# Selective scan beside full attention: some products with C move to VectorE, which sums them over a unit

## The chip, the cores and the metric

The kernel runs on one core of a Trainium2 chip. The metric is the time of one execution in device microseconds. The engines of the core are named as in the profile: PE (TensorE, matrix products), DVE (VectorE), ACT (ScalarE), POOL (GpSimd) and SP (SyncE, which here issues most of the DMAs).

## The reference

A tensor of 8 images, 64 channels, 64 x 64 pixels passes through four layers: full attention over all 4096 pixels of an image, two blocks of windowed attention, a convolution with filters made from the data, and a layer around a selective scan. Two pieces matter here. The attention of layer 0:

```python
scores = jnp.einsum('bdn,bdm->bnm', Q, Q) / c ** 0.5      # 4096 x 4096 per image
prob = jax.nn.softmax(scores, axis=-1)
out = jnp.einsum('bnm,bdm->bdn', prob, V)
```

And the scan of layer 3, over 4096 positions in four directions k, with 16 states n for each of 128 channels:

```python
def step(h, inp):
    u_t, dt_t, B_t, C_t = inp
    h = h * jnp.exp(dt_t[..., None] * A) + dt_t[..., None] * B_t[:, :, None, :] * u_t[..., None]
    return (h, jnp.einsum('bkcn,bkn->bkc', h, C_t))
```

The output y of a position is thus the sum over 16 states of h times C. All numbers are fp32.

## The kernel before, in words

**Pairs and what runs together.** The images are taken in four pairs p. `tile_kernel` (lines 1906 to 1915) calls `scans(p, ...)` for each pair and gives it other work to run beside it: the back stage of pair p-1 (`back`, after the scan) and the front stage of pair p+1 (`front`: layers 0, 1 and 2 and the sources of the scan). Layer 0 of pairs 0 and 1 is done before the first scan, in `begin`. So full attention (`layer0`, lines 1291 to 1320) runs beside the scan only twice: that of pair 2 beside the scans of pair 1, and that of pair 3 beside the scans of pair 2.

**The scan.** A unit is one image, one direction k and one chunk c of 512 positions: 2 x 4 x 8 = 64 units a pair, of 8 steps each, and a step holds two states, j = 0 and 1. So a pair has 512 steps. The directions of an image are numbered in order by `nth`, 0 to 3.

- `inputs` (line 1688) loads the unit's xs by DMA on SP, makes the step sizes and u (lines 1697 to 1704: two ACT passes, a DVE product) and writes the rows of B and C to memory. It is called for the next unit during step 1 of a unit.
- `fetch` (1712) loads a step's rows of B and C, broadcast to 128 partitions, on SP, with three buffers each. `products` (1719) has GpSimd multiply B with u into `vd`, which has six buffers.
- `step` (1724): for each state ACT makes the decay `dad` in PSUM (line 1743; tag "da", three buffers, shared with what `inputs` needs); DVE scans (1746), either into `hd` in SBUF or in place into `dad`; ACT copies the last column into `carry` (1754); and the product with C is written to `vd` (1757 or 1760). `own`, line 1732, says how many of a step's two products DVE makes, those of the last states. GpSimd makes the others, [...] only DVE's own states are scanned in place. For pairs 0 to 2 `own` is 0 in even steps (one GpSimd product of 1024 elements) and 1 in odd ones; for pair 3 it is 1, in every fourth step 2.
- `sums` (1764) adds the 16 products of a unit in one PSUM bank `yd` (tag "y", one buffer) by multiplying each with the identity on PE (line 1775), one step behind, and placed by `net.behind` after the next step's product `st["w"]`. After the eighth step DVE takes the bank into `Y` (1784, 1786), or for `nth` 3 into `yo` (1789, one buffer), which is stored by a DMA on SP (1790).

**The attention.** For each chunk jc of 512 columns, 32 blocks t: for both images of the pair PE makes scores (1305) into PSUM banks "f" (three buffers), ACT takes their exponential into `e` (1311, six buffers), and PE multiplies the previous block's `e` with the values into `po` (1297, one bank). DVE copies `po` out after the 32 blocks (1320).

**The order.** Each piece of beside-work yields a cost: 2.2 for one block t, 4 for one of the 8 groups of values before the loop. `scans` lets it advance, after each step, by an equal share of the planned cost over 512 - 24 steps (line 1681). The planned cost is that of the front stage (its yields add up to 2016) and a quarter of it for the back stage (whose yields add up to 264.4). This sets the order in which instructions are written. The framework then orders them for each engine by priority and readiness at compile time and adds the semaphores. A tile whose buffer is taken waits for the last use of the tile that had it. [...]

Of the kernel before, what the change touches and what calls it, by code (L numbers as in the profile page):

```python
# [9 lines left out]
F32 = mybir.dt.float32  # L10
AF = mybir.ActivationFunctionType
ALU = mybir.AluOpType
# [3 lines left out]
B, C, HH, WW = 8, 64, 64, 64  # L16
L = HH * WW
P = 128
# [6 lines left out]
TD = 512  # L25
# [1132 lines left out]
class _Direct:  # L1158
# [8 lines left out]
    def __init__(self, net, ctx):  # L1167
        self.net, self.tc, self.nc, self.w = net, net.tc, net.nc, net.w
        tc = self.tc
        self.dram = ctx.enter_context(tc.tile_pool(name="mem", bufs=2, space=bass.MemoryType.DRAM))  # L1170
        self.slabs = ctx.enter_context(tc.tile_pool(name="slabs", bufs=3))
        self.ps = ctx.enter_context(tc.tile_pool(name="ps_scan", bufs=3, space=PSUM))
        self.pf = ctx.enter_context(tc.tile_pool(name="ps_front", bufs=3, space=PSUM))
        self.kept = {}
        self.turn = -1

    def begin(self, ctx):

# [91 lines left out]
    def layer0(self, p):  # L1270


        nc, tc, w, net, half = self.nc, self.tc, self.w, self.net, self.HALF
        X = self.flat("X")
        nc.sync.dma_start(X, self.net.x[2 * p : 2 * p + 2].rearrange("b c h w -> (b c) (h w)"))
        att = self.padded("att")
        VT = self.flat("VT").rearrange("p (t c) -> p t c", c=P)

        def at(rows, t):
            return X[rows, t * P : (t + 1) * P]  # L1280

        with self.work("w0") as wk:
            for g in range(8):
                pv = self.bank("pval", (P, 4, P))
                nc.tensor.matmul(pv, lhsT=net.ones[0:1, :], rhs=net.b1row.rearrange("o a c -> o (a c)").unsqueeze(1).to_broadcast([1, 4, P]), start=True, stop=False)
                for j in range(4):
                    nc.tensor.matmul(pv[:, j, :], lhsT=at(slice(0, P), 4 * g + j), rhs=net.w1bd, start=False, stop=(j == 3))
                nc.scalar.activation(VT[:, 4 * g : 4 * g + 4, :], pv, AF.Relu)
                yield 4

            parts = wk.tile([P, 2, 32, NCH], F32, name="parts", tag="parts", bufs=1)
            for jc in range(NCH):
                po = self.total("po")

                def weigh(t, es):
                    for im in range(2):
                        nc.tensor.matmul(  # L1297
                            po[half[im]], lhsT=VT[:, t, half[im]], rhs=es[im], start=(t == 0), stop=(t == 31)
                        )

                last = None
                for t in range(32):
                    ss = [self.bank(f"s{im}") for im in range(2)]
                    for im in range(2):
                        nc.tensor.matmul(  # L1305
                            ss[im], lhsT=at(half[im], t), rhs=X[half[im], jc * CH : (jc + 1) * CH], start=True, stop=True
                        )
                    es = []
                    for im in range(2):
                        e = wk.tile([P, CH], F32, name="e", tag="e", bufs=6)  # L1310
                        nc.scalar.activation(  # L1311
                            e, ss[im], AF.Exp, scale=C**-0.5, accum_out=parts[:, im, t, jc : jc + 1]
                        )
                        es.append(e)
                    if last is not None:
                        weigh(*last)
                    last = (t, es)
                    yield 2.2
                weigh(*last)
                nc.vector.tensor_copy(self.rows(att, jc), self.img(po))  # L1320

            sums = net.sums[:, p]
            nc.vector.tensor_reduce(sums, parts, AX.X, ALU.add)
            rec = wk.tile([P, 2, 32], F32, name="rec", tag="rec", bufs=1)
            nc.vector.reciprocal(rec, sums)
            for g in range(8):
                pr = self.bank("prec")
                for j in range(4):
                    for im in range(2):
                        nc.tensor.matmul(  # L1330
                            pr[half[im], j * P : (j + 1) * P],
                            lhsT=rec[:, im, 4 * g + j : 4 * g + j + 1].to_broadcast([P, 64]),
                            rhs=w["ident"],
                            start=True,
                            stop=True,
                        )
                d = self.rows(att, g)
                nc.vector.tensor_tensor(d, d, self.img(pr), ALU.mult)
                yield 4
        with self.work("w0b") as wk:  # L1340
            for c in range(NCH):
                acc = self.bank("cacc", (P, 8, 64))
                yield from self.dwconv(acc, att, 8 * c, 8, w["dw2"], None)
                cv = wk.tile([P, 8, 64], F32, name="cv", tag="cv")
                nc.scalar.activation(cv, acc, AF.Relu, scale=net.bn23[:, 0:1], bias=net.bn23[:, 1:2])
                pw = self.bank("pw")
                nc.tensor.matmul(pw, lhsT=w["w3bd"], rhs=cv, start=True, stop=True)
                t = wk.tile([P, CH], F32, name="t", tag="t")
                nc.scalar.activation(t, pw, AF.Identity, scale=net.bn23[:, 2:3], bias=net.bn23[:, 3:4])
                x = X[:, c * CH : (c + 1) * CH]  # L1350
                nc.vector.tensor_tensor(x, x, t, ALU.add)
                yield 3
        return X
# [370 lines left out]
    def step(self, i, st):  # L1724

        nc, w, net = self.nc, self.w, self.net
        wk, ps = self.sw, self.ps
        u = self.units[i // 8]
        k, c, at, CC, v = u["k"], u["c"], u["at"], st["C"], st["v"]

        n0 = 2 * (i % 8)
        own = 1 + (i % 4 == 3) if u["image"] >= B - 2 else i % 2
        rev = k >= 2

        def along(t):
            return t[:, ::-1] if rev else t

        h = wk.tile([P, 2 - i % 2, TD], F32, name="hd", tag=f"h{i % 2}", bufs=1)
        hs = []
        for j in range(2):  # L1740
            n = n0 + j
            da = self.bank("dad", (P, TD), "da")
            nc.scalar.activation(da, u["du"][:, 0], AF.Exp, scale=net.As[:, k, n : n + 1])  # L1743
            first = 0.0 if at == 0 else self.carries[:, n : n + 1]
            to = da if j >= 2 - own else h[:, j]
            nc.vector.tensor_tensor_scan(along(to), along(da), along(v[:, j]), first, ALU.mult, ALU.add)  # L1746
            hs.append(to)
            if at < NTD - 1 and (own or j):
                ends = h[:, :, 0] if rev else h[:, :, TD - 1]
                cs = self.carries[:, n0 : n0 + 2]  # L1750
                if own:
                    ends = to[:, 0:1] if rev else to[:, TD - 1 : TD]
                    cs = self.carries[:, n : n + 1]
                nc.scalar.activation(cs, ends, AF.Copy)  # L1754

        if own == 0:
            st["w"] = nc.gpsimd.tensor_tensor(v, h, CC, ALU.mult)  # L1757
        for j in range(2 if own else 0):
            engine = nc.vector if j >= 2 - own else nc.gpsimd
            m = engine.tensor_tensor(v[:, j], hs[j], CC[:, j], ALU.mult)  # L1760
            if j == 0:
                st["w"] = m

    def sums(self, i, st, after=None):

# [1 line left out]
        wk, ps = self.sw, self.ps  # L1767
        u = self.units[i // 8]
        k, c = u["k"], u["c"]
        if i % 8 == 0:  # L1770
            u["y"] = ps.tile([P, TD], F32, name="yd", tag="y", bufs=1)
        y = u["y"]
        for j in range(2):
            n = 2 * (i % 8) + j
            m = nc.tensor.matmul(y, lhsT=w["ident"], rhs=st["v"][:, j], start=(n == 0), stop=(n == NST - 1))  # L1775
            if after is not None and j == 0:
                net.behind(m, after)
        if i % 8 < 7:
            return

        yd = net.part(self.Y, k, c)
        yp = y.rearrange("p (a b) -> p a b", b=64)
        if u["nth"] == 0:
            nc.vector.scalar_tensor_tensor(yd, self.img(u["x"]), net.dsum, yp, ALU.mult, ALU.add)
        elif u["nth"] < 3:
            nc.vector.tensor_tensor(yd, yd, yp, ALU.add)
        else:
            o = wk.tile([P, TD], F32, name="yo", tag="yo", bufs=1)
            nc.vector.tensor_tensor(self.img(o), yd, yp, ALU.add)
            nc.sync.dma_start(u["out"][:, c * TD : (c + 1) * TD], o)  # L1790

# [155 lines left out]
```

## Time and profile before

| | |
|---|---|
| runs, median (lowest to highest) | 13679.33 us (13679.1 to 13687.01) |
| the profiled execution, its time | 13724.29 us |
| its span | 13722.5 us |
| its mean granted PE clock | 0.88 |
| busy in the span | PE 11044.8, DVE 8484.9, ACT 7083.5, POOL 8012.5 us |
| sums on PE (line 1775) | 8192 instructions, 4620.1 us |
| products with C, POOL, 1024 elements (1757) | 768, 2358 ns each |
| products with C, POOL, 512 elements (1760) | 1152, 1280 ns each |
| products with C, DVE, 512 elements (1760) | 1408, 674 ns each |
| scans, DVE (1746), the largest group | 2352, 1271 ns each |
| store of `yo`, issue to landing | 64, 2.4 us median |

An fp32 matrix product appears as two matmul instructions. Busy time is the time in which an engine had an instruction under way; instructions of PE overlap at their ends. A slice of the page is a fortieth of the span, 343 us, and its digit the busy share in tenths. In a group or a timeline, "out<-in" names the tiles written and read; "idle before, releaser" says what ended the time in which the engine stood still.

### The profile page before, as it was taken

Reading aid. Unit: us, or ns where it says so; the run is one execution under the profiler, and the core shown is the slowest. Engines: PE = TensorE matmul, PEld = TensorE weight load, DVE = VectorE, ACT = ScalarE, POOL = GpSimd, SP = SyncE. Lnnn points to the kernel's source line nnn. Section 1 sums busy time; section 2 is a strip of 40 time slices with the busy share of each in tenths; the row PEclk is TensorE's granted clock in tenths of the full one; section 3 lists DMA queues with packets and bytes.
Section 4 is the critical chain, followed back from the end, with each engine's and each line's share of the span. In section 5 each row is a group of like instructions: output and inputs, shape, how many; then the busy total and the mean of one; then the engine's idle time right before and its main releaser. Section 6 shows DMA issues by size and latency. Waiting matters only on the chain. (4 is left out here: it accounts for less than half of the span.)

```text
span 13722.5 us, 141112 instructions
## 1 busy us (share of the span) xinstructions
PE 11044.8 (80%) x46358; PEld 4075.2 (30%) x46358; DVE 8484.9 (62%) x9891; ACT 7083.5 (52%) x15475; POOL 8012.5 (58%) x3983
## 2 busy tenths in 40 slices
PE   9999986888786669979888677997898766766665
PEld 2243322334232222224432222223453222222221
DVE  0121336777668673366666766337666778998985
ACT  5556515565536545555554545555554554454442
POOL 0000005888878754566666785556656687877882
PEclk9999977998898889988898788998889888888887
DMA  0000005666667753454555664435545577778882
GB/s 24 1 1 1 3 14 191 237 236 229 219 214 253 248 170 129 143 173 165 173 176 181 234 242 149 139 134 184 182 160 171 192 247 262 270 241 278 294 298 97
DMA packets 706252, 2385.19 MB, mean 174 GB/s; under 512 B 81120, under 2 KB 81248, under 8 KB 704480
## 3 DMA queue, kind: packets, MB, share of 16 engines
q1 hardware_dynamic: 681312, 2319.76, 49.5%
q10 hardware_dynamic: 24192, 56.29, 1.1%
q8 instruction: 367, 6.01, 0.2%
q14 instruction: 381, 3.12, 0.1%
HBM read 2272.97 MB, written 102.76 MB: 173 GB/s over the span
## 5 line engine op out<-in xcount | busy, mean ns | idle before, releaser
L1722 POOL TENSOR_TENSOR vd<-B,du 128x1024 f32<-128x1024 f32 x2048 | 4833.6, 2367 | 3890.9 <-DMA B<-rows 2485.1
L1775 PE MATMUL yd<-vd,pack 128*128 128x512 f32 x8192 | 4620.1, 695 | 1323.4 <-POOL vd L1757 576.6
L1746 DVE TENSOR_TENSOR_SCAN hd<-dad,carry,vd 128x512 f32<-128x512 f32 x2352 | 2948.5, 1271 | 933.8 <-ACT dad L1743 483.4
L1743 ACT ACTIVATE dad<-du,As 128x512 f32<-128x512 f32 x4096 | 2721.0, 680 | 1142.8 <-DVE hd L1746 730.6
L1775 PEld LDWEIGHTS yd<-vd,pack 128*128 128x128 f32 x8192 | 1621.4, 214 | 3993.6 <-issue 1786.3
L1757 POOL TENSOR_TENSOR vd<-hd,C 128x1024 f32<-128x1024 f32 x768 | 1810.6, 2358 | 1204.1 <-DVE hd L1746 599.6
L1311 ACT ACTIVATE e<-s 128x512 f32<-128x512 f32 x2048 | 1199.9, 591 | 1012.2 <-PE s L1305 1010.4
L1760 POOL TENSOR_TENSOR vd<-hd,C 128x512 f32<-128x512 f32 x1152 | 1473.8, 1280 | 339.7 <-DVE hd L1746 281.1
L1746 DVE TENSOR_TENSOR_SCAN dad<-dad,carry,vd 128x512 f32<-128x512 f32 x1232 | 1562.0, 1274 | 124.4 <-POOL vd L1722 73.2
L1305 PE MATMUL s<-X 64*128 64x512 f32 x4096 | 1324.4, 648 | 79.7 <-ACT e L1311 79.5
L1297 PE MATMUL po<-e,VT 128*64 128x512 f32 x4096 | 1194.9, 627 | 13.2 <-ACT e L1311 13.2
L1760 DVE TENSOR_TENSOR vd<-dad,C 128x512 f32<-128x512 f32 x1408 | 939.3, 674 | 66.5 <-ACT carry L1754 57.7
L1754 ACT ACTIVATE carry<-hd 128x1 f32<-128x1 f32 (+1 forms) x1680 | 334.8, 202 | 1012.0 <-DVE hd L1746 1007.8
L1305 PEld LDWEIGHTS s<-X 64*128 64x128 f32 x4096 | 360.1, 187 | 958.9 <-issue 785.8
L1459 PEld LDWEIGHTS w_av<-vals,w_e 64*64 64x64 f32 x16384 | 556.6, 147 | 195.7 <-issue 84.3
L1459 PE MATMUL w_av<-vals,w_e 64*64 64x9 f32 x16384 | 584.7, 208 | 25.7 <-ACT w_e L1449 25.5
L1444 DVE TENSOR_TENSOR w_e<-w_s,bias 128x512 f32<-128x512 f32 x512 | 329.8, 682 | 443.1 <-PE w_s L1432 442.2
L1754 ACT ACTIVATE carry<-dad 128x1 f32<-128x1 f32 x1232 | 208.7, 169 | 697.7 <-DVE dad L1746 695.1
L1697 PE MATMUL pdd<-xs,xdt 128*128 128x512 f32 x512 | 341.7, 755 | 205.5 <-DVE hd L1746 85.8
L1449 ACT ACTIVATE w_e<-w_e 128x512 f32<-128x512 f32 x512 | 311.6, 627 | 376.2 <-DVE w_e L1444 262.2
L1746 DVE TENSOR_TENSOR_SCAN hd<-dad,vd 128x512 f32<-128x512 f32 x336 | 400.5, 1211 | 164.5 <-ACT dad L1743 75.5
L1297 PEld LDWEIGHTS po<-e,VT 128*64 128x64 f32 x4096 | 221.4, 136 | 822.1 <-issue 771.9
(247 smaller groups left out, 10634.9 us busy)
## 6 DMA issues: line engine op xcount, KB each, us to landing
B<-rows SPq DMA_DIRECT2D x2048, 512.0 KB, 5.0
C<-rows SPq DMA_DIRECT2D x2048, 512.0 KB, 4.5
xs<-xt SPq DMA_DIRECT2D x128, 256.0 KB, 3.3
xs<-xc SPq DMA_DIRECT2D x128, 256.0 KB, 3.8
xc<-xcv ACTq DMA_DIRECT2D x64, 256.0 KB, 3.4
zs<-z ACTq DMA_DIRECT2D x64, 256.0 KB, 3.6
xt<-XT ACTq DMA_DIRECT2D x32, 512.0 KB, 7.6
rows<-bc SPq DMA_DIRECT2D x256, 64.0 KB, 1.8
```

Of the source, the lines that this page charges most:

```text
L1297: nc.tensor.matmul(po[half[im]], lhsT=VT[:, t, half[im]], rhs=es[im], start=(t == 0), stop=(t == 31))
L1305: nc.tensor.matmul(ss[im], lhsT=at(half[im], t), rhs=X[half[im], jc * CH : (jc + 1) * CH], start=True, stop=True)
L1311: nc.scalar.activation(e, ss[im], AF.Exp, scale=C**-0.5, accum_out=parts[:, im, t, jc : jc + 1])
L1459: nc.tensor.matmul(self.av[half[im], x % 4 + j, h, :], lhsT=es[h // 4][half[im], j, h % 4, :], rhs=V[half[im], x + j, h, :], start=True, s ...
L1697: nc.tensor.matmul(pd, lhsT=net.xdt[:, k, :], rhs=x, start=True, stop=True)
L1722: self.nc.gpsimd.tensor_tensor(v, st["B"], dx.to_broadcast([P, 2, TD]), ALU.mult)
L1743: nc.scalar.activation(da, u["du"][:, 0], AF.Exp, scale=net.As[:, k, n : n + 1])
L1746: nc.vector.tensor_tensor_scan(along(to), along(da), along(v[:, j]), first, ALU.mult, ALU.add)
L1754: nc.scalar.activation(cs, ends, AF.Copy)
L1757: st["w"] = nc.gpsimd.tensor_tensor(v, h, CC, ALU.mult)
L1760: m = engine.tensor_tensor(v[:, j], hs[j], CC[:, j], ALU.mult)
L1775: m = nc.tensor.matmul(y, lhsT=w["ident"], rhs=st["v"][:, j], start=(n == 0), stop=(n == NST - 1))
```

## The change

A flag `dense` is 1 while the loop of full attention over jc is being written, else 0. Steps written with the flag set have `own` one higher: in even steps GpSimd makes one product and VectorE one, in odd steps VectorE makes both. So three of each four products are VectorE's. In these steps VectorE's products no longer go into `vd` for PE. The first of a unit is written to a new tile `ysum` (one buffer, SBUF); each later one is written over its state in `dad` in PSUM and then added to `ysum` by a second VectorE instruction. `to_y` lists what PE still has to sum: GpSimd's products, and at the unit's eighth step `ysum`. The accumulation on PE begins with the first of these. Separately, and in all units with `nth` 3, the tile `yo` is gone: the output is written over the unit's xs tile (two buffers) and stored from there.

```diff
@@ layer0
             parts = wk.tile([P, 2, 32, NCH], F32, name="parts", tag="parts", bufs=1)
+            self.dense = 1
             for jc in range(NCH):
...
+            self.dense = 0
             sums = net.sums[:, p]
@@ step
-        own = 1 + (i % 4 == 3) if u["image"] >= B - 2 else i % 2
+        own = 1 + (i % 4 == 3) if u["image"] >= B - 2 else i % 2 + self.dense
...
         for j in range(2 if own else 0):
-            engine = nc.vector if j >= 2 - own else nc.gpsimd
-            m = engine.tensor_tensor(v[:, j], hs[j], CC[:, j], ALU.mult)
-            if j == 0:
-                st["w"] = m
+            if j < 2 - own or not self.dense:
+                engine = nc.vector if j >= 2 - own else nc.gpsimd
+                m = engine.tensor_tensor(v[:, j], hs[j], CC[:, j], ALU.mult)
+            elif "sum" not in u:
+                s = u["sum"] = wk.tile([P, TD], F32, name="ysum", tag="ysum", bufs=1)
+                m = nc.vector.tensor_tensor(s, hs[j], CC[:, j], ALU.mult)
+            else:
+                m = nc.vector.tensor_tensor(hs[j], hs[j], CC[:, j], ALU.mult)
+                nc.vector.tensor_tensor(u["sum"], u["sum"], hs[j], ALU.add)
+            st.setdefault("w", m)
+        st["to_y"] = [v[:, j] for j in range(2) if not self.dense or j < 2 - own]
+        if i % 8 == 7 and "sum" in u:
+            st["to_y"].append(u["sum"])
@@ sums
-        if i % 8 == 0:
-            u["y"] = ps.tile([P, TD], F32, name="yd", tag="y", bufs=1)
-        y = u["y"]
-        for j in range(2):
-            n = 2 * (i % 8) + j
-            m = nc.tensor.matmul(y, lhsT=w["ident"], rhs=st["v"][:, j], start=(n == 0), stop=(n == NST - 1))
+        srcs = st["to_y"]
+        for j, v in enumerate(srcs):
+            start = "y" not in u
+            if start:
+                u["y"] = ps.tile([P, TD], F32, name="yd", tag="y", bufs=1)
+            stop = i % 8 == 7 and j == len(srcs) - 1
+            m = nc.tensor.matmul(u["y"], lhsT=w["ident"], rhs=v, start=start, stop=stop)
             if after is not None and j == 0:
                 net.behind(m, after)
...
-            o = wk.tile([P, TD], F32, name="yo", tag="yo", bufs=1)
+            o = u["x"]
             nc.vector.tensor_tensor(self.img(o), yd, yp, ALU.add)
             nc.sync.dma_start(u["out"][:, c * TD : (c + 1) * TD], o)
```

More of the change, by code (lines that the diff above doesn't have):

```diff
@@ L1320, in layer0 @@
                 nc.vector.tensor_copy(self.rows(att, jc), self.img(po))
+            self.dense = 0
             sums = net.sums[:, p]
@@ L1779, in sums @@
             return
+        y = u["y"]
         yd = net.part(self.Y, k, c)
```

## The prediction

> **What bounds the kernel now.** I read the page first (engine shares, slices, largest groups), then the busy time of each engine in 500 us windows, then the windows in which the full attention runs beside the scan, and there the groups, the waits and the timeline. The change acts only there, so that stage decides and not the average.
>
> The page, engines by slice:
>
> ```profile
> PE   9999986888786669979888677997898766766665
> DVE  0121336777668673366666766337666778998985
> PEclk9999977998898889988898788998889888888887
> ```
>
> Slices 15 to 17 and 25 to 27 stand out: PE at 9 while VectorE falls to 3. The score matmuls of the attention (line 1305) run from 5084.4 to 5980.6 and from 8428.4 to 9321.8 us there. Windows cut at these places (columns: busy time and count of PE, weight load, DVE, ACT, POOL; then clock, DMA share, GB/s):
>
> ```profile
> 5084.40:5983.90 899.50, 853.40 (x2542) 232.62 (x2542) 334.27 (x317) 511.35 (x1466) 456.85 (x222) 0.97 0.40 135
> 8394.40:9323.00 928.60, 878.76 (x2643) 246.67 (x2643) 351.16 (x333) 522.15 (x1485) 482.36 (x235) 0.97 0.41 141
> ```
>
> PE is busy 95% of the first stage, DVE 37%, ACT 57%, POOL 51%. The same windows for line 1775 alone, the summing matmuls with the identity:
>
> ```profile
> 5084.40:5983.90 899.50, 227.55 (x438) 78.18 (x438) 0.97 0.40 135
> 8394.40:9323.00 928.60, 240.34 (x464) 82.22 (x463) 0.97 0.41 141
> ```
>
> A quarter of PE's time is this sum. One fp32 product is two matmul instructions, so 219 products in 227.55 us: 1.04 us each. 219 is 109.5 steps of two products, which agrees with the planned costs (below). Who waits, in the first stage:
>
> ```profile
> ACT e L1311 <- PE s L1305: 270.7, 160, 5.5
> POOL vd L1722 <- PE yd L1775: 268.0, 57, 8.2
> DVE Y L1786 <- PE yd L1775: 230.5, 12, 26.9
> ...
> PE s L1305 <- ACT e L1311: 39.4, 27, 3.5
> ```
>
> ACT, POOL and DVE all wait for PE, DVE up to 26.9 us in one piece; PE waits 39.4 us for ACT and hardly for anything else. PE's timeline where nothing disturbs it:
>
> ```profile
> 5599.55 1.13 PE L1305 MATMUL s<-X 64*128 64x512 f32 x4
> 5600.61 1.08 PE L1297 MATMUL po<-e,VT 128*64 128x512 f32 x4
> 5601.62 1.13 PE L1305 MATMUL s<-X 64*128 64x512 f32 x4
> ...
> 5609.74 1.12 PE L1697 MATMUL pdd<-xs,xdt 128*128 128x512 f32 x2
> 5610.80 1.04 PE L1706 MATMUL pbc<-xs,pack 128*32 128x512 f32 x2
> 5611.77 1.13 PE L1305 MATMUL s<-X 64*128 64x512 f32 x4
> ```
>
> One block t of the attention takes 2.07 us (start to start), the inputs of a unit 2.03 us. So a stage needs at least 256 x 2.07 = 530, plus 218 sums x 0.99 = 216 (the timeline's block of two lasts 1.98), plus 14 x 2.03 = 28: 774 us. It takes 899.5. The 125 us between are PE's losses: waits for ACT and stretches at a lower clock.
>
> [...]
>
> **The change part by part.**
>
> *Which steps.* A pair's plan is 504 + 2016 = 2520 cost over 488 steps, 5.164 a step. The attention's loop costs 256 x 2.2 = 563.2, hence 109 steps, and begins after 264.4 for the back stage and 32 for the values: the flag holds in steps 58 to 166 of pairs 1 and 2, units 7 to 20. Pairs 0 and 3 never see it.
>
> *Removed on PE.* A whole unit has 5 products (4 from GpSimd, one for the sum) in place of 16; the first and last unit are partly flagged. Counted over steps 58 to 166: 149 products fewer per pair, 149 x 1.04 = 155 us. PE sets the stage's end, so this counts in full: 899.5 - 155 = 744.5.
>
> *Moved to VectorE.* VectorE's products rise from 54 to 163, +109 x 0.674 = 73 us. 149 additions and 14 first products into the sum; the nearest row for the addition is line 1789 (PSUM plus SBUF into SBUF), 678 ns: 101 us. The product is now written to PSUM; scans into PSUM (1274 ns) and into SBUF (1271) say that costs nothing. The dearest bound for both is line 1786 with its strided operand, 1064 ns; then the addition's group alone grows to 159 us. VectorE goes from 334 to 509 us of about 745, 68%: covered by PE, with 236 us of slack. Without that cover the 175 us would be paid in full.
>
> *GpSimd.* 54 products of 512 go (1.27 us) and 55 shrink from 2.35 to 1.27: -128 us, 457 to 329. It was waiting anyway; worth nothing.
>
> *ScalarE.* An even step copies two carries separately where it copied one pair: some 48 more copies of 0.17 to 0.2 us, 9 us a stage. ScalarE goes to 520 of 745, 70%. Here I charge something. The sum blocks, 2 us each, are where ScalarE does the scan's exponentials without delaying the attention's: after a score pair it has 2.07 - 1.26 = 0.8 us free, and one exponential takes 0.68. With fewer sum blocks more of them fall into the attention's own loop, and PE waits. I let the 125 us of losses grow as ScalarE's share, 70/57: +29 us a stage. Ends: losses 40 lower, since the scan's bursts are spread wider by VectorE's longer work, to 100 higher.
>
> *The new waits.* The sum tile has one buffer. VectorE's first product of a unit waits until PE has consumed the previous unit's sum; behind it on VectorE's queue stand the scans, for which ScalarE (three PSUM buffers) waits, and behind that the attention's exponentials. PE's sum in turn waits for the unit's last addition. VectorE already meets PE once a unit at the Y update, up to 26.9 us early, so this meeting is mostly the same one. A unit holds VectorE for 16 x 1.27 + 12 x 0.674 + 11 x 0.678 + 2 = 38 us against PE's 47 at its floor: 9 us of slack; I put nothing on it beyond the 29.
>
> *Output from the xs buffer.* In 64 units the result is written over xs and stored from there. The load of xs two units on now waits for that store to land (2.4 us median), and on SP's queue the B and C loads stand behind it. In the trace the xs load often follows the store by 1 to 4 us, and its consumer comes 10 us later or more, so 1 us or so each is late and mostly covered. Bounds 0 to 64 x 2.4 = 154 us; I take 5.
>
> *Sum.* 2 x (155 - 29) - 5 = 247 us. Against the profiled execution: 13722.5 - 247 = 13475 span. That execution (13724.3 with what lies around the span) is 45 us above the runs' median 13679.33, 0.33%; I carry the difference over: 13679 - 247 = 13432, say 13430.
>
> **Rivals.**
>
> *A, PE-bound stage, as summed.* 13310 to 13500. The lower end: each stage's losses fall by 30 us in place of growing by 29, 370 off; the upper: they grow by 60 to 65.
>
> *B, ScalarE and the clock take half.* If PE waits at every scan exponential (109 x 2 x 0.5 us = 109 a stage less what already waits) or the clock falls from 0.97 to 0.88, as in windows with 84% PE (745 x 0.1 = 75 us a stage), the gain is about 2 x 70: 13540. For it: the 25 us window from 5620 to 5645, in the thick of a burst, has PE at 85% and clock 0.88. Against: 5410 to 5440, with ACT at 70%, has PE at 96% and clock 1.00.
>
> *C, slower: the meeting at the sum tile serialises.* If PE reaches the sum with VectorE's chain unfinished and everything stands, a unit pays part of the 38 us on top of its 47. It decides at about 11.5 us a unit (2 x 155 / 27): at 20 us a unit the result is 13679 - 309 + 27 x 20 = 13910. Against: PE is the late one today at every unit.
>
> *D, no change*: the stage's pace is not PE's but something that all waits hide. 268 and 230 us of waits for PE speak against it.
>
> **How the numbers follow.** A 0.65, B 0.22, C 0.08, D 0.05. What a measurement can tell is 0.2%, 27 us. 8 in 10: from 13310 to 13580, which holds A and most of B. Faster: A and B, 0.87; same: D, 0.05; slower: C, 0.08.
>
> **What would show it.** yd products 8192 to about 7596 instructions; POOL 128x1024 products with C from 768 to 658; about 298 additions of 0.68 us and 28 products into the sum tile; the two stages at about 770 us each, PE still above 90%, clock at least 0.95, DVE about 65%. Other stages the same length. The prediction is wrong if the stages stay above 850, if PE waits long for DVE at the sum, or if the part from 11000 us on, which sees only the xs edit, grows by over 30 us.

## The result, and the profile after

The changed kernel took 13526.34 us (median of four runs, 13523.46 to 13549.57) against 13683.17 for the kernel before (13679.1 to 13703.24): a ratio of 0.9886, 95% interval 0.9869 to 0.9903. It is faster by 157 us in the medians; the forecast was 247 (13430 us), with a range of 13310 to 13580. The profiled executions, 13722.5 and 13547.6 us of span, differ by 175, and these are compared below. They lie 41 and 23 us above the medians, so that this difference comes out a little larger.

The page of the changed kernel, engines by slice:

```profile
PE   9999986888787669989888667997898666666665
DVE  0121236776668676676666767667675768988985
PEclk9999977998898779999889788998888788888887
```

Beside the attention VectorE stood at 3 in four slices before (two in each of the two stretches, not three as the forecast has it); there it is now at 6 or 7. The attention's score products run from 5145.6 to 5897.1 and from 8354.4 to 9105.5 us. Windows cut there (time and count of PE, weight load, DVE, ACT, POOL, then clock, DMA share, GB/s):

```profile
5145.60:5899.00 753.40, 731.87 (x2242) 190.88 (x2242) 486.37 (x573) 510.04 (x1514) 332.29 (x168) 0.99 0.49 161
8354.40:9107.00 752.60, 730.99 (x2237) 189.64 (x2238) 486.19 (x572) 509.53 (x1510) 332.28 (x168) 0.99 0.49 162
```

The same windows for the summing products alone:

```profile
5145.60:5899.00 753.40, 77.47 (x139) 20.60 (x138) 0.99 0.49 161
8354.40:9107.00 752.60, 77.43 (x139) 20.60 (x138) 0.99 0.49 162
```

PE is still the engine that sets the pace (97% busy, clock 0.99); the sum fell from 227.55 to 77.47 us. The groups of VectorE's new work in the first stage (count, busy us, mean ns, then idle time before):

```profile
L1771 DVE TENSOR_TENSOR ysum<-ysum,dad 128x512 f32<-128x512 f32 x149 | 100.0, 671 | 0.9
L1770 DVE TENSOR_TENSOR dad<-dad,C 128x512 f32<-128x512 f32 x149 | 98.3, 682 | 3.0 <-ACT carry L1758 2.8
```

And who waits there (us in total, times, longest):

```profile
POOL vd L1725 <- PE yd L1789: 166.5, 29, 10.9
ACT e L1313 <- PE s L1307: 138.9, 110, 3.4
...
DVE ysum L1768 <- PE yd L1789: 118.1, 13, 12.2
...
PE s L1307 <- ACT e L1313: 14.5, 22, 1.6
```

VectorE's meeting with PE has moved from the Y update (12 waits, 230.5 us) to the sum tile (13 waits, 118.1 us), and PE still waits for nobody long.

So each stage is shorter than forecast: from the first to the last score product 896.2 and 893.8 us became 751.5 and 751.1, together 287 us less. But the span fell by 175 only. The rest of the span is the riddle of this case:

| | first stage | second stage | all else | span |
|---|---|---|---|---|
| before | 896.2 | 893.8 | 11932.5 | 13722.5 |
| after | 751.5 | 751.1 | 12045.0 | 13547.6 |

112 us were lost outside the stages: 61 of them ahead of the first one (its first score product starts at 5145.6 in place of 5084.4), 10 between the two, 41 after. Ahead of the first stage the flag is never set beside a scan; of the change only the output written over xs is there. What it does can be seen in the first units with `nth` 3. The timeline of the kernel before:

```profile
3101.66 1.74 SPq L1694 DMA_DIRECT2D xs<-xc  x2
...
3129.28 0.32 SPq L1790 DMA_DIRECT2D ys<-yo  x1
...
3133.40 1.02 PE L1697 MATMUL pdd<-xs,xdt 128*128 128x512 f32 x2
```

And of the changed kernel at the same place:

```profile
3131.48 0.32 SPq L1805 DMA_DIRECT2D ys<-xs  x1
...
3133.55 0.32 SPq L1697 DMA_DIRECT2D xs<-xc  x1
3133.98 0.38 SPq L1720 DMA_DIRECT2D C<-rows  x1
3134.77 1.59 SPq L1720 DMA_DIRECT2D B<-rows  x2
...
3138.98 2.07 PE L1700 MATMUL pdd<-xs,xdt 128*128 128x512 f32 x2 [1.11 <-DMA xs<-xc]
```

Before, xs was loaded some 30 us ahead of its first use (two loads in a row, the second issued by 3103.40, and the next first use at 3133.40). Now the load is issued 2.07 us after the store of the tile that had its buffer, and PE's first product waits for it: the lead is 5.4 us. Over all 64 units with `nth` 3 the median lead, from the issue of the load to the first product, fell from 51.9 to 5.7 us. That SP holds the load back for the store stands in the waits of SP's queue after the change, and in no line of those before (us in total, times, longest):

```profile
SPq L1697 <- DMA ys<-xs: 96.3, 56, 5.9
```

The waits for xs at the first product of a unit in the whole span (products and weight loads counted each; of the products alone 70 us before and 159 after), before:

```profile
  DMA xs<-xt: 52.3, 31
  DMA xs<-xc: 49.7, 15
```

and after:

```profile
  DMA xs<-xc: 166.6, 53
  DMA xs<-xt: 68.8, 43
```

The stores of consecutive units with `nth` 3 lie 39.3 us apart before and 41.8 after (mean over the eight stretches of eight units).

### The profile page after: what moved, and what is told of

Read it like the earlier page. It is cut to its first block, busy times and chain, and to the rows that moved or that the text cites. A ratio compares the mean times of both kernels' runs of the same rounds, so it can differ in the third digit from the quotient of the medians.

```text
span 13547.6 us, 140341 instructions
## 1 busy us (share of the span) xinstructions
PE 10802.4 (80%) x45762; PEld 3981.2 (29%) x45762; DVE 8783.4 (65%) x10407; ACT 7087.6 (52%) x15569; POOL 7764.9 (57%) x3875
## 5 line engine op out<-in xcount | busy, mean ns | idle before, releaser
L1789 PE MATMUL yd<-vd,pack 128*128 128x512 f32 x7540 | 4263.8, 696 | 1381.0 <-POOL vd L1761 591.9
L1750 DVE TENSOR_TENSOR_SCAN hd<-dad,carry,vd 128x512 f32<-128x512 f32 x2166 | 2713.2, 1270 | 677.8 <-ACT dad L1747 385.9
L1789 PEld LDWEIGHTS yd<-vd,pack 128*128 128x128 f32 x7540 | 1497.0, 215 | 3843.5 <-issue 1654.4
L1761 POOL TENSOR_TENSOR vd<-hd,C 128x1024 f32<-128x1024 f32 x658 | 1551.4, 2358 | 1068.2 <-DVE hd L1750 702.0
L1750 DVE TENSOR_TENSOR_SCAN dad<-dad,carry,vd 128x512 f32<-128x512 f32 x1418 | 1793.3, 1274 | 160.3 <-POOL vd L1725 99.1
L1313 ACT ACTIVATE e<-s 128x512 f32<-128x512 f32 x2048 | 1200.7, 591 | 751.1 <-PE s L1307 749.6
L1299 PE MATMUL po<-e,VT 128*64 128x512 f32 x4096 | 1226.7, 621 | 12.6 <-ACT e L1313 9.9
L1765 DVE TENSOR_TENSOR vd<-dad,C 128x512 f32<-128x512 f32 x1300 | 864.9, 672 | 48.2 <-ACT carry L1758 39.1
L1758 ACT ACTIVATE carry<-dad 128x1 f32<-128x1 f32 x1422 | 240.9, 169 | 804.1 <-DVE dad L1750 801.4
L1574 PE MATMUL acc<-tap,pack 128*128 128x512 f32 x576 | 367.5, 761 | 99.5 <-DVE tap L1573 98.1
```

What stands on the lines that cost most here:

```text
L1299: nc.tensor.matmul(po[half[im]], lhsT=VT[:, t, half[im]], rhs=es[im], start=(t == 0), stop=(t == 31))
L1313: nc.scalar.activation(e, ss[im], AF.Exp, scale=C**-0.5, accum_out=parts[:, im, t, jc : jc + 1])
L1574: nc.tensor.matmul(acc, lhsT=w["ident"], rhs=tap, start=(t == 0), stop=(t == TAPS - 1))
L1789: m = nc.tensor.matmul(u["y"], lhsT=w["ident"], rhs=v, start=start, stop=stop)
```

## The experiments

The stages, the rest and the waits are read from one profiled execution of each kernel. Executions of one kernel lie up to 73 us apart in time (e2_own_yo: 13397.89 to 13471.07), and the two stages of e2_own_yo differ by 4 us.

Theory: (1) in the two stages PE sets the time, and the summing products taken from it are the gain; (2) the xs edit costs some 110 us, by the next load's wait for the store. Rivals: the loss outside the stages comes from another order of the instructions, which the flag causes; the gain comes from what leaves GpSimd, not from what leaves PE.

### The xs edit alone

```diff
 # kernel before
-            o = wk.tile([P, TD], F32, name="yo", tag="yo", bufs=1)
+            o = u["x"]
```

> The kernel before with one edit: the output of nth 3 is written over xs and stored from there, no flag and no sum tile. Theory (the xs edit delays the next xs load behind the store's landing, some 1.8 us in each of 64 units, and PE then waits for xs): 13790 us, 90 to 140 above before, and PE's waits for xs at the pdd product rise from 102 to about 235 us. Rival (the 112 us lost outside the two attention stages come from another order of the instructions, which the new flag causes): within 30 us of before.

Measured: 13824.74 us against 13686.35, ratio 1.0102 (1.0083 to 1.0120). In the profile the stages are as before (897.0 and 893.7 us), and all else takes 12046.3, within 2 us of the changed kernel's 12045.0. The waits at the first product of a unit:

```profile
  DMA xs<-xc: 172.6, 49
  DMA xs<-xt: 70.0, 42
```

The edit alone makes the kernel slower by 1%, and it accounts for the whole loss outside the stages. The rival falls.

### The change without the xs edit

The output tile takes the buffer of the sum tile: the flag is set in units 7 to 20 only, whose `nth` is 0 to 2.

```diff
 # changed kernel
-            o = u["x"]
+            o = wk.tile([P, TD], F32, name="yo", tag="ysum", bufs=1)
```

> The changed kernel, but the output of nth 3 keeps a tile of its own, which shares its buffer with the sum tile (the two are never in use in the same units). Theory: the two attention stages stay at 751 us each, the rest returns to its length of before: 13683 - 2 x 144 = 13395 us. Rival (order): about 13526, as the changed kernel.

Measured: 13425.14 us, ratio 0.9819 (0.9791 to 0.9847), which is near what had been forecast for the whole change. Stages 752.3 and 756.6 us, all else 11912.1 (11932.5 before). In the profile the span is 301 us shorter than before; in the medians it is 261 us, where 288 had been expected.

### The products moved, PE's sum kept

```diff
 # e2_own_yo
-            if j < 2 - own or not self.dense:
+            if True:
...
-        st["to_y"] = [v[:, j] for j in range(2) if not self.dense or j < 2 - own]
+        st["to_y"] = [v[:, j] for j in range(2)]
```

> As e2_own_yo, but VectorE's products go into vd and PE sums all 16 of a unit, so that VectorE makes three of four products and PE saves nothing. Theory (PE's summing is what set the stage): each attention stage 890 to 910 us, total 13660 to 13720. Rival (the gain came from taking products off GpSimd and freeing the vd buffers sooner): stages clearly shorter than 896, total near 13530 or lower.

Measured: 13647.02 us, ratio 0.9971 (0.9963 to 0.9979). Stages 873.4 and 872.4 us, somewhat below the theory's 890 to 910. So of the 144 us by which a stage is shorter, about 22 come already with the products moved, and the other 120 or so with what PE no longer sums. The rival holds for a sixth of the gain. Why the moved products help at all was not settled: PE's work is the same, and it loses less between its instructions (108 us in the first stage in place of 131, counted as below).

### All products on VectorE but one a unit

```diff
 # e2_own_yo
-        own = 1 + (i % 4 == 3) if u["image"] >= B - 2 else i % 2 + self.dense
+        own = 1 + (i % 4 == 3) if u["image"] >= B - 2 else max(i % 2, self.dense * (1 + (i % 8 > 0)))
```

> As e2_own_yo, but in steps with the flag VectorE makes both products, except in the first step of a unit: PE keeps 2 of 16 products a unit in place of 5. Theory (PE still bounds the shortened stage): some 40 products fewer a stage at 1.04 us, stages about 710, total 13310. Rival (ScalarE or VectorE now sets the pace of the stage): stages 740 or longer, total no better than e2_own_yo.

Measured: 13352.01 us, ratio 0.9763 (0.9746 to 0.9779). Stages 723.5 and 722.8 us. The first window (columns as above):

```profile
5069.40:5794.50 725.10, 712.11 (x2157) 189.47 (x2156) 528.02 (x652) 505.19 (x1505) 278.35 (x125) 1.00 0.51 167
```

PE is 98% busy and VectorE 73%. 42 products fewer a stage than in e2_own_yo, 43 us at 1.04, made the stages 29 and 34 us shorter: PE still bounds the stage, with a little lost.

### A third buffer for xs

```diff
 # e1_xs_only
-        x = u["x"] = wk.tile([P, TD], F32, name="xs", tag="xs")
+        x = u["x"] = wk.tile([P, TD], F32, name="xs", tag="xs", bufs=3)
```

> As e1_xs_only (the output written over xs, stored from there), but with three xs buffers in place of two, which take the place of the dropped output tile. Theory (the cost of the xs edit is the next load's wait for the store to land): the next loads find a free buffer, and the time returns to that of before, 13660 to 13710 us; PE's waits for xs fall back to about 100 us. Rival (writing the output over xs costs by itself, or by another order): it stays near 13825.

Measured: 13606.23 us, ratio 0.9923 (0.9904 to 0.9942): not only back to the time before but 0.8% below it. All else takes 11851.9 us, the waits at the first product of a unit are

```profile
  DMA xs<-xc: 63.5, 21
  DMA xs<-xt: 26.6, 19
```

and the stores of units with `nth` 3 lie 39.6 us apart. SP's waits for the store fell by about half:

```profile
SPq L1694 <- DMA ys<-xs: 50.8, 18, 5.4
```

Where the time goes is seen when the whole span is cut at the ends of the units (the VectorE instruction that takes the bank) and summed by `nth`, in us:

```
nth               0        1        2        3
before       2891.2   3027.9   2827.6   2491.3
e1_xs_only   2865.2   3071.4   2762.9   2654.5
e6_xs_three  2785.9   3008.9   2826.6   2510.4
```

The xs edit alone lengthens the units with `nth` 3 by 163 us (the others together become 47 shorter); with three buffers 19 of the 163 are left. So writing the output over xs costs little by itself; the missing buffer does. What lies below the kernel before is in the units with `nth` 0, 105 us. They read xs once more at their end (line 1784), so the kernel before holds its buffer that long there too. SP's waits for that in the kernel before:

```profile
SPq L1694 <- DVE Y L1784: 154.3, 51, 14.6
```

and with three buffers:

```profile
SPq L1694 <- DVE Y L1784: 101.3, 20, 15.0
```

The median lead of the load in these units rose from 7.2 to 27.5 us. The same memory (two xs tiles and one output tile, or three xs tiles) is worth more as three xs tiles. The theory had the mechanism; that the kernel before pays for it too, and that the time would end below it, was not foreseen.

### ScalarE's share in PE's losses: less work, more work, other banks

A count of the timeline shows what PE loses in a stage. A row is a run of the same product without a pause over 0.15 us; counted is the time to the next row's start less the undisturbed step (0.26 us an instruction of the scores, 0.25 of the values, 0.5 of all others). In the first stage:

```
before         130.5 us   score rows of two instructions: 80 with 84.2 us;  of four: 207 with 14.3
after          134.8 us   score rows of two instructions: 49 with 42.1 us;  of four: 222 with 45.1
attention alone, 62 to 600 us of the kernel before: 20.8 us
```

The scores of the two images are made from different halves of the 128 partitions (`half[im]` in the kernel, 64*128 in the trace). Issued together they are a row of four instructions and take 1.13 us; apart they are two rows of two, 1.12 us each (medians of the first stage before). Of some 40 blocks whose scores are apart in the kernel before, PE pauses between the halves in 26, which fits its 27 waits for an exponential to free a bank (`PE s L1305`, 39.4 us); in 13 a summing product stands between them in PE's queue. Three runs asked what holds them up. No carries:

```diff
 # e2_own_yo
-            first = 0.0 if at == 0 else self.carries[:, n : n + 1]
+            first = 0.0 if at == 0 or self.dense else self.carries[:, n : n + 1]
...
-            if at < NTD - 1 and (own or j):
+            if at < NTD - 1 and (own or j) and not self.dense:
```

> As e2_own_yo, but in steps with the flag ScalarE copies no carries and the scans start from zero, so that the states of those chunks lack what came before them. It takes some 190 copies of 0.17 to 0.2 us a stage, and their waits for VectorE (66 us), off ScalarE's queue. Theory (PE's losses of some 125 us a stage come from score products that wait for ScalarE's exponentials, held up by other ScalarE work): stages fall from 752 to 700 to 735 us. Rival (the losses are the clock's or VectorE's): stages within 8 us of 752.

Measured (one profiled execution): stages 739.3 and 748.7 us, 13 and 8 less than in e2_own_yo, beyond the rival's bound on the first and within it on the second, and short of what the theory expected. One exponential more:

```diff
 # e2_own_yo
+            if j == 1 and own == 1 and self.dense:
+                nc.scalar.activation(h[:, 1], u["du"][:, 0], AF.Exp, scale=net.As[:, k, n : n + 1])
             first = 0.0 if at == 0 else self.carries[:, n : n + 1]
```

> As e2_own_yo, with one exponential more of 512 elements on ScalarE in every even step with the flag (55 a stage, 0.68 us each, 37 us of ScalarE's time; its result is not used). Theory (ScalarE's other work in the attention's stretch holds up the exponentials of the scores and so PE): stages longer than 752 to 757 us by 15 to 40. Rival (ScalarE has room; the losses have another cause): stages within 6 us.

Measured (one profiled execution): stages 757.3 and 755.9 us against 752.3 and 756.6. The first window of e2_own_yo, then that of this run (ACT is the fourth pair of numbers):

```profile
5074.00:5828.00 754.00, 732.46 (x2239) 190.35 (x2239) 486.41 (x572) 509.97 (x1513) 332.15 (x168) 0.99 0.50 161
5077.50:5836.50 759.00, 736.17 (x2237) 190.41 (x2238) 486.89 (x572) 540.74 (x1566) 332.44 (x168) 0.98 0.50 160
```

31 us more of ScalarE's time cost the stage at most 5, no more than the two stages of e2_own_yo differ: the rival is right, and busy time of ScalarE to this amount is not what PE loses by. Other banks:

```diff
 # e2_own_yo
-        self.ps = ctx.enter_context(tc.tile_pool(name="ps_scan", bufs=3, space=PSUM))
-        self.pf = ctx.enter_context(tc.tile_pool(name="ps_front", bufs=3, space=PSUM))
+        self.ps = ctx.enter_context(tc.tile_pool(name="ps_scan", bufs=2, space=PSUM))
+        self.pf = ctx.enter_context(tc.tile_pool(name="ps_front", bufs=4, space=PSUM))
```

> As e2_own_yo, with four PSUM banks for the scores (and the rest of the beside-work) and two for the scan's decays, in place of three and three. Only the attention stages are read. Theory (PE loses time because the two halves of a score pair do not find both banks free and run one after the other): fewer score products in rows of two instructions than 54, stages below 735 us. Rival (the scan with two banks paces everything in the stage, or the banks don't matter): stages at 750 us or longer.

Measured (one profiled execution): stages 749.5 and 750.0 us. The score rows of two instructions in the first stage fell from 51 (the expectation took 54) to 13, as the theory said, but the value products (`po`), which need the exponentials, came apart in their place: 55 rows of two, with 38 us, where there had been 14 with 10. The wait has moved, and the stage is only 3 to 7 us shorter. With two banks for the decays ScalarE's exponentials of the scan wait more for VectorE to free one, in this run

```profile
ACT dad L1747 <- DVE ysum L1771: 59.9, 64, 3.0
```

and in e2_own_yo

```profile
ACT dad L1747 <- DVE ysum L1771: 30.0, 41, 2.8
```

and the attention's exponentials stand behind them in ScalarE's queue. That these waits, rather than busy time, make up the rest of PE's losses fits all three runs but was not isolated. It stays open.

### The flag through the windowed attention too

```diff
 # e5_all_dve, in front(); the reset after the loop over jc is dropped
+        self.dense = 1
         yield from self.layer1(X)
+        self.dense = 0
 # in step(): the flag counts in units with nth 1 and 2 only
+        dn = self.dense and u["nth"] in (1, 2)
```

> As e5_all_dve, but the flag stays set through layer 1 (windowed attention), in all pairs that run it beside the scan, in units with nth 1 or 2. Theory (taking sums off PE pays only where PE is the late one; in the windowed stage PE is 84 to 89% busy and VectorE 70%, and the two meet closely): within 60 us of e5_all_dve either way. Rival (PE bounds the windowed stage as well): 100 us or more below e5_all_dve.

Measured: 13580.72 us, ratio 0.9907 (0.9888 to 0.9926), which is 229 us above e5_all_dve (some 200 by the two ratios), worse than either expected. Stages of full attention 730.6 and 730.7. More than half of the loss, 149 of 258 us of span, is beside pair 0's scan. The window from 2300 to 3300 us in e5_all_dve:

```profile
2300.00:3300.00 1000.00, 836.23 (x5962) 378.53 (x5966) 757.33 (x871) 567.42 (x1143) 876.57 (x429) 0.91 0.70 236
```

and with the flag, followed by PE's largest wait there:

```profile
2300.00:3300.00 1000.00, 610.48 (x4506) 296.15 (x4505) 868.56 (x1133) 497.85 (x1025) 544.11 (x255) 0.67 0.61 201
PE w_ot L1487 <- DVE w_o L1479: 122.2, 17, 16.4
```

Here VectorE was at 76% before anything was added. With the additions it reaches 87%, PE falls from 84 to 61%, and PE's granted clock from 0.91 to 0.67; PE waits 122.2 us for this product of VectorE in the windowed attention, up to 16.4 at a time, where it had been 15.7 and up to 4.7. The same edit that pays beside full attention costs here.

### The two findings together

```diff
 # e5_all_dve
-        x = u["x"] = wk.tile([P, TD], F32, name="xs", tag="xs")
+        x = u["x"] = wk.tile([P, TD], F32, name="xs", tag="xs", bufs=3)
...
-        bc = wk.tile([2 * NST, TD], F32, name="bc", tag="bc")
+        bc = wk.tile([2 * NST, TD], F32, name="bc", tag="bc", bufs=1)
```

> As e5_all_dve with three xs buffers (one buffer fewer for the rows of B and C, to make room). If the early xs loads are worth here what e6_xs_three showed over before (0.8%), 13240 to 13290 us; if they were worth it only there, or the single buffer of rows takes it back, 13350 as e5_all_dve.

Measured: 13264.35 us against 13704.04, ratio 0.9687 (0.9672 to 0.9703): 3.1% faster than the kernel before, and the fastest version of the study. Stages 715.3 us each, all else 11831.9.

All runs side by side. Lengths are of one profiled execution each; of e7, e9 and e10 there is only this one, and no ratio:

```
                first   second  all else  span      ratio of times (95%)
before          896.2   893.8   11932.5   13722.5   1
after           751.5   751.1   12045.0   13547.6   0.9886 (0.9869-0.9903)
e1_xs_only      897.0   893.7   12046.3   13837.0   1.0102 (1.0083-1.0120)
e2_own_yo       752.3   756.6   11912.1   13421.0   0.9819 (0.9791-0.9847)
e4_move_only    873.4   872.4   11905.3   13651.1   0.9971 (0.9963-0.9979)
e5_all_dve      723.5   722.8   11867.5   13313.8   0.9763 (0.9746-0.9779)
e6_xs_three     887.9   880.8   11851.9   13620.6   0.9923 (0.9904-0.9942)
e7_no_carry     739.3   748.7   11902.5   13390.5   -
e8_windows_too  730.6   730.7   12110.6   13571.9   0.9907 (0.9888-0.9926)
e9_more_act     757.3   755.9   11883.9   13397.1   -
e10_banks       749.5   750.0   12045.4   13544.9   -
e11_best        715.3   715.3   11831.9   13262.5   0.9687 (0.9672-0.9703)
```

## Why the prediction was right, and which terms were off

**The stage and its bound: right.** PE sets the time beside full attention, before and after. That what leaves PE makes most of the gain is shown by e2_own_yo against e4_move_only: 121 and 116 us of the 144 a stage.

**Removed on PE: right.** 149 products fewer a pair: 596 matmul instructions, 8192 to 7540 + 56 (the sums of `ysum` are a group of their own). The sum on PE fell by 150 us in the first stage; 155 had been worked out at 1.04 us a product.

**VectorE's new work: right.** 149 additions at 671 ns and 149 products into PSUM at 682 ns, where 678 and 674 had been taken; VectorE is at 65%. Written to PSUM the product took 8 ns more than the 674 of the one into `vd`, and less than the 691 of a unit's first one into `ysum`, so the place it is written to costs nothing that counts. (Line 1786, the dearest bound, took 975 ns in the mean over the span before and 1087 in its first stage, not 1064; that its strided operand is the cause was not shown.) The single sum tile did not serialise anything (rival C): PE waits 2.3 us or less at a time for the exponentials, and of its waits for VectorE in the first stage none is over 0.8 us. (A unit's floor on PE comes to 46 us from the forecast's own figures, not 47, which changes nothing.)

**ScalarE's term: too high.** I charged 29 us a stage because ScalarE's share would rise, and it did, from 57 to 68%. The losses hardly grew, from 130.5 to 134.8 us. The step that failed is "I let the 125 us of losses grow as ScalarE's share"; e9_more_act shows that even 31 us more of ScalarE's time cost 5 at most. The stage is accounted for without it: 149 products at their undisturbed 0.99 us are 147.5, less 4 of added losses 143, and 144.7 and 142.7 were measured. So the stages fell by 144 in place of 126: 35 us more gain over both than the sum had. What holds up the score products, the largest part of the losses, stays open.

**The xs edit: far too low, and this is the term by which the forecast came out 96 us too fast.** "I take 5", of bounds 0 to 154; it measured 114 in the profile by itself (e1_xs_only) and 1.0% of the time. The mechanism had been named, the load's wait for the store to land. The step that failed is "mostly covered". SP waited for the store 96.3 us in 56 loads, 1.7 us each where 1 had been taken, and this was not covered. The cover was misread in the trace: in the kernel before 13 loads follow a store within some 4 us, and 11 of these are used 5.6 to 8.7 us after their issue, not 10 or more. And the cover that mattered was how long xs was loaded before its first use, 52 us in the median of the units with `nth` 3, of which the edit left 5.7. What stands behind xs on SP's queue had been named and not priced: in about half of the units with `nth` 3 the loads of B next behind it are those of the unit's steps 5 and 6, and for these GpSimd waited 99 us in the changed kernel where it had waited 38. Whether this or PE's own wait for xs sets the loss was not isolated. In the terms of the forecast: 2 x 144 - 112 = 176 off the profiled execution, where 2 x (155 - 29) - 5 = 247 had been summed. That the time still fell into the stated range owes something to luck: the gain of the stages was taken 35 us too small and the cost of the xs edit 107 us too small, and in part these cancel.

**Rivals.** The time, 13526, lies above A (to 13500) and near B (13540), but not by B's mechanism (ScalarE and the clock take half): the clock rose from 0.97 to 0.99 and the stages did better than A's sum. Without the xs edit the time falls into A (e2_own_yo, 13425). The xs edit as a loss of its own stood in no rival. The forecast had named the sign by which this would be seen, growth of the part from 11000 us on by over 30 us. From the end of the unit that ends there before the change, the rest of the span grew from 2718 to 2773 us, and from the last score product on it grew from 4400 to 4442: by the forecast's own sign the term for xs was wrong.

## What to carry to other kernels

Moving a sum off the engine that sets a stage's pace paid nearly its full time here (144 us of a stage for 150 us of PE's, some 22 of them by the move alone), and cost where the receiving engine was already close (VectorE at 76% before the additions of e8_windows_too): find the stage first, and switch the work by stage. A small edit that merges two tiles to save memory can undo a good part of it: ask of a merged tile how long before its use the next content used to be loaded, and which loads stand behind it in the queue, not how long a single wait is. And when memory is short, try which tile the last 2 KB serve best: here the output tile's memory, given to xs as a third buffer, made the kernel 0.8% faster than before, because the units with `nth` 0 had been holding xs to their end as well.

## What the runs showed of the hardware

Two score products from different halves of the 128 partitions run at the same time when they are issued together: in the first stage of the kernel before, four instructions took 1.13 us, and two alone 1.12. Beside the scan about a sixth of the blocks lost this (80 rows of two instructions before, two to a block), at about 1 us a row, and that made 84 of PE's 131 us of losses. PE's granted clock was 0.67 in the window of e8_windows_too from 2300 to 3300 us, where PE was 61% busy, 0.97 in the two stages of the kernel before, where it was 95% busy, 0.99 in those of the changed kernel (97%), and 1.00 in the first stage of e5_all_dve (98%).
